# A hand-written issue order for the layer part of a fused decoder kernel

## The chip, the core and the metric

The kernel runs on one core of one Trainium2 chip. The metric is device time in microseconds (us) of one execution; lower is better. A core has five instruction streams that matter here: TensorE (PE in the profile, with its weight loads as PEld), VectorE (DVE), ScalarE (ACT), GpSimd (POOL) and SyncE (SP), which issues most of the transfers. Each stream is worked off in the order in which its instructions stand, and semaphores make one stream wait for another.

## The reference

The input is `x` of shape 8 x 512 x 512 (batch, sequence, width) in 32-bit floats. Three sublayers follow each other, each inside a residual sum and a layernorm:

```python
x = _layernorm(x + mamba(x))                    # _L0_attn_ref
x = _layernorm(x + cross_attention(x, ctx))     # _L0_xattn_ref, 16 heads of 32
x = _layernorm(x + mixture_of_experts(x))       # _L0_ffn_ref, 32 experts, 4 for each token
```

The first is a state-space layer: layernorm, projection to two halves of 1024 channels, a causal convolution of four taps with silu on one half, a projection to `dt`, `B` and `C`, `dt = softplus(...)`, and then for every one of 1024 channels and 16 states the recurrence along the sequence

```python
h = dA_t * h + dBx_t                      # dA = exp(A * dt),  dBx = dt * B * x
y_t = einsum('bdn,bn->bd', h, C_t)
```

followed by a gate with silu of the other half and a projection back to 512. The second is cross attention with softmax over 512 keys. The third routes each token to 4 of 32 experts (each with room for 640 tokens), adds a shared expert, and sums.

## The kernel before

`program` calls three functions, one after the other. `layers` (lines 83 to 1121) does the first two sublayers, the routing and the shared expert; `experts` does the 32 experts; `finish` does the last layernorm. Only `layers` is touched by the change.

**Chunks and steps.** `layers` walks over 16 chunks: 8 batches, 2 chunks of 256 positions each. A chunk has 32 steps, `steps = [(q, g, i) ...]`: channel pair `q`, state group `g`, and one of two channel blocks. I number the steps of a batch 0 to 63. One step holds one piece of the recurrence: `carry` copies the four starting states into `h` (ScalarE, L443); `decays` computes the four exponentials for the next step into one of two buffers `das` (ScalarE, L437); `scan` multiplies (VectorE, L449), runs the scan (VectorE, L453) and saves the end state (L455); `collect` multiplies the states by C (VectorE, L470) and sums over them on TensorE (L474).

**Other work in the same step.** Before `collect`, a step also emits part of the work that prepares the next chunk or finishes the last one: projections with the streamed weights `wm` (L302), the output projection `back` (L503) with its layernorm, the convolution taps (L336), softplus for the next channel pair (`prepare`, L389 to L412), and two runs of silu, each with two loads of ScalarE's function table (L353, L354). It further emits items of a list `side`: the cross attention, the routing and the shared expert of the batch before, and the keys and values of the batch after. An item has a weight, and the list is spread evenly over a batch's steps by these weights. In attention, `maximum` computes scores (L766) and VectorE reduces them (L768); `weigh` computes them again, transposed (L792), and ScalarE exponentiates (L796); `gather` multiplies with the values (L808). The scores of L766 and L792 share two PSUM buffers (pool `l_pss`).

**Work and clearing away.** An item emits its matmuls at once and returns what empties its PSUM result; that is emitted one item later:

```python
    def do(fn, *args, first=False):
        if first:
            dry()
        rest = fn(*args)
        settle()
        if rest:
            left.append(rest)
```

The body of a step, shortened:

```python
            h = carry(t, 2 * q + ci, g)
            ...
                decays(2 * nq + ni, ng, (f if k + 1 < len(steps) else nf)["ready", nq][0], das[(n + 1) % 2])
            scan(t, 2 * q + ci, g, f["ready", q][1], bc, das[n % 2], h)
            ...
            settle()
            collect(2 * q + ci, g, h, bc, py, f)
```

What stands at the `...` between `scan` and `settle()` are the `do` calls of that step. The `settle()` ahead of `collect` empties everything that is still pending, so that in the source all clearing away of a step stands ahead of its L470.

**What sets the order.** The kernel is written against a recording layer that has a scheduler: the source order is a priority, and the scheduler places each instruction of each engine by its own estimate of when inputs and buffers are ready. A few instructions are tied to the source order by hand (`tc.keep_in_program_order` on the silus of L353 and L354). Transfers on SP (weights, the broadcasts `bc` of L378, the rearranged `both` of L418, the attention's small copies) are placed by the scheduler too.

**Buffers named below.** `h` has 4 buffers, `das` 2, `wm` 3 and `wa` (the attention and shared-expert weights, L525) 2; `both` has 2 for each of its two tiles, `bc` 6; `cT`, the context of the next batch (L661), shares one buffer with the attention's output. `xr` (L725), rows of the first sublayer's result, has 2.

Of the kernel before, what the change touches and what calls it, by code (L numbers as in the profile page):

```python
# [1422 lines left out]
def program(tc, a, out):  # L1423
    nc = tc.nc
    with tc.tile_pool(name="dram", bufs=1, space=DRAM) as dram:
        x1d = dram.tile([N, D], F32, name="x1d")
        filld = dram.tile([B, S], F32, name="filld")

        based = dram.tile([N + P, D], F32, name="based")
        xbuf = dram.tile([SLOTS, ROW], F32, name="xbuf")  # L1430
        nc.scalar.preload_act_table_set(LN_EXP)

        with ExitStack() as ctx:
            layers(ctx, tc, a, x1d, filld, based, xbuf)
        with ExitStack() as ctx:
            experts(ctx, tc, a, xbuf, based)
        with ExitStack() as ctx:
            finish(ctx, tc, based, out)
# [31 lines left out]
```

## Time and profile before

| | |
|---|---|
| median of 3 runs | 5567.89 us (5564.01 to 5571.6) |
| the profiled execution: its own time, its span | 5569.36 us, 5567.7 us |
| TensorE busy | 4880.6 us (88%) |
| VectorE busy | 4349.5 us (78%) |
| ScalarE busy | 2592.1 us (47%) |
| GpSimd busy | 569.2 us (10%) |
| first and last start of the scan L453 | 72.2 and 3688.8 us |
| first expert matmul (L1220) | 3963.3 us |

Busy shares are means over the whole span. The kernel has three stretches with different loads: the steps, from 72 to 3692 us; the attention and shared expert of the last batch alone, to 3963 us; experts and last layernorm, to the end. A matmul's duration in the profile overlaps that of its neighbours, so where I need the cost of an operation I use the distance between starts in the timeline.

### The profile page before, as it was taken

The page shows a single profiled execution, that of the slowest core. Times are in us where ns is not written, and L with a number is a line of the kernel's source. Part 1 is how long each engine was busy: PE and PEld are TensorE (multiplying, and loading weights), DVE is VectorE, ACT ScalarE, POOL GpSimd, SP SyncE. Part 2 cuts the span into 40 slices and gives each one's busy share as a digit, 9 for nine tenths or more (in the row PEclk, how much of TensorE's full clock was granted, in tenths as well). Part 3 has the DMA queues.
Part 4 walks back from the last instruction along what each step waited for, and adds up shares of the span by engine and source line. Part 5 has one row for each costly group of instructions (what it writes and reads, how often), then busy time and mean ns, then how long its engine had stood idle before and what let it go on. Part 6 is the DMA issues. An engine that isn't in the chain of part 4 may idle for free. (4 is left out here: it accounts for less than half of the span.)

```text
span 5567.7 us, 60361 instructions
## 1 busy us (share of the span) xinstructions
PE 4880.6 (88%) x19752; PEld 2718.5 (49%) x19752; DVE 4349.5 (78%) x5738; ACT 2592.1 (47%) x5481; POOL 569.2 (10%) x424
## 2 busy tenths in 40 slices
PE   6668889888888988888898898879899999999994
PEld 4334344334434434443443443333577777777773
DVE  6998899989889999898989999864466565555554
ACT  4555555655566455555555656523222222222223
POOL 1000002001100200200020020010111111111111
PEclk8778999999999999999999999989999999999997
DMA  6787355444634634643463454441345454544444
GB/s 187 226 229 211 109 137 176 121 118 143 178 106 112 201 97 129 184 124 108 122 207 98 120 188 113 112 158 45 96 125 126 124 126 119 126 125 120 119 121 145
DMA packets 554282, 769.83 MB, mean 138 GB/s; under 512 B 135754, under 2 KB 268394, under 8 KB 551920
## 3 DMA queue, kind: packets, MB, share of 16 engines
q1 hardware_dynamic: 517952, 677.55, 41.6%
q0 software_dynamic: 33280, 76.90, 7.4%
q10 hardware_dynamic: 2736, 11.54, 0.5%
q8 instruction: 156, 2.56, 0.2%
q14 instruction: 158, 1.29, 0.1%
HBM read 508.68 MB, written 165.05 MB: 121 GB/s over the span
## 5 line engine op out<-in xcount | busy, mean ns | idle before, releaser
L437 ACT ACTIVATE l_da<-both,l_aneg 128x256 f32<-128x256 f32 x2048 | 888.4, 499 | 790.6 <-DVE h L453 745.9
L453 DVE TENSOR_TENSOR_SCAN h<-l_da,h 128x1028 f32<-128x1028 f32 x512 | 1170.0, 2292 | 50.7 <-ACT h L443 27.3
L474 PE MATMUL py<-h,l_twice 128*64 128x256 f32 x4096 | 627.5, 421 | 195.1 <-DVE h L470 194.9
L449 DVE TENSOR_TENSOR h<-both,bc 128x1024 f32<-128x1024 f32 x512 | 617.9, 1214 | 142.5 <-PE py L474 81.6
L470 DVE TENSOR_TENSOR h<-h,bc 128x1024 f32<-128x1024 f32 x512 | 622.6, 1219 | 6.3 <-DMA l_ka<-filld 0.3
L474 PEld LDWEIGHTS py<-h,l_twice 128*64 128x64 f32 x4096 | 292.5, 147 | 568.8 <-issue 237.7
L1220 PE MATMUL ps_h<-xT,w 128*128 128x320 f32 x1536 | 435.6, 433 | 0.0
L766 PE MATMUL ps_s<-l_ka,l_qa 64*128 64x512 f32 x1024 | 314.1, 692 | 137.4 <-DVE mx L768 137.2
L1300 POOL DMA_INDIRECT based<-y,xe x160 | 252.1, 1576 | 1313.5 <-ACT y L1323 571.3
L1241 DVE TENSOR_TENSOR hT<-ps_h,p 128x320 f32<-128x320 f32 x128 | 62.9, 492 | 379.0 <-PE ps_h L1220 379.0
L768 DVE TENSOR_REDUCE mx<-ps_s 128x2 f32<-128x1024 f32 x256 | 310.4, 1216 | 55.4 <-PE ps_s L766 54.7
L1220 PEld LDWEIGHTS ps_h<-xT,w 128*128 128x128 f32 x1536 | 292.2, 190 | 118.2 <-issue 0.4
L792 PE MATMUL ps_t<-l_qa,l_ka 64*128 64x512 f32 x1024 | 299.6, 648 | 20.9 <-ACT eT L796 17.5
L796 ACT ACTIVATE eT<-ps_t 128x1024 f32<-128x1024 f32 x256 | 259.1, 1013 | 110.1 <-PE ps_t L792 109.6
L808 PE MATMUL po<-eT,l_va 128*64 128x512 f32 x1024 | 281.4, 629 | 24.5 <-ACT raw L820 20.8
L641 POOL DMA_INDIRECT xbuf<-x2t,dest x128 | 218.8, 1709 | 814.6 <-DVE dest L635 776.2
L1220 PE MATMUL ps_h<-t,s 128*128 128x320 f32 x1024 | 286.1, 432 | 0.0
L302 PE MATMUL ps_z<-xnT,wm 128*128 128x256 f32 x1024 | 240.9, 389 | 17.4 <-DVE o L512 16.4
L302 PE MATMUL ps_x<-xnT,wm 128*128 128x256 f32 x1024 | 245.6, 394 | 11.1 <-DMA wm<-in_in_proj_w 10.1
L703 PE MATMUL ps_p<-x2T,wa 128*128 128x512 f32 x512 | 243.9, 625 | 11.8 <-DVE hT L883 10.3
L503 PE MATMUL po<-wm,zs 128*128 128x512 f32 x512 | 236.9, 613 | 9.8 <-DVE k L688 5.3
L1220 PEld LDWEIGHTS ps_h<-t,s 128*128 128x128 f32 x1024 | 194.6, 190 | 81.1
(234 smaller groups left out, 7422.5 us busy)
## 6 DMA issues: line engine op xcount, KB each, us to landing
bc<-scr SPq DMA_DIRECT2D x1024, 128.0 KB
w<-in_w SPq DMA_DIRECT2D x93, 1024.0 KB
wm<-in_in_proj_w SPq DMA_DIRECT2D x128, 512.0 KB
xbuf<-zero SPq DMA_DIRECT2D x32, 1362.5 KB
xe<-xbuf SPq DMA_DIRECT2D x32, 1362.5 KB
both<-dt SPq DMA_DIRECT2D x256, 128.0 KB
both<-dtx SPq DMA_DIRECT2D x256, 128.0 KB
wm<-in_out_proj_w SPq DMA_DIRECT2D x64, 512.0 KB
```

Source lines behind the costliest of these rows:

```text
L302: nc.tensor.matmul(ps[:, i, :], w[:, dc, i * P : (i + 1) * P], f["xnT"][:, dc, :], start=(dc == 0), stop=(dc == DC - 1),)
L437: nc.scalar.activation(da[:, n, 1:], dt[:, c % 2, j, :], AF.Exp, scale=aneg[:, c, j, g, m : m + 1])
L449: nc.vector.tensor_tensor(steps, dtx[:, c % 2].unsqueeze(2).to_broadcast([P, 2, NG // 2, T]), bc[0], ALU.mult)
L453: nc.vector.tensor_tensor_scan(flat, da.rearrange("p n t -> p (n t)"), flat, 0.0, ALU.mult, ALU.add)
L470: nc.vector.tensor_tensor(steps, steps, bc[1], ALU.mult)
L474: nc.tensor.matmul(py[j * HP : (j + 1) * HP, c % 2, :], twice, h[:, j * 2 + m, 1:], start=False, stop=(s == (NST // NG - 1, NG // 2 - 1, 1)),)
L766: nc.tensor.matmul(ps[:, j, :], qa[r, lt * P : (lt + 1) * P], ka[r, :], start=True, stop=True)
L768: return lambda: nc.vector.tensor_reduce(mx[:, lt, :].unsqueeze(2), ps, AX.X, ALU.max) and None
L792: nc.tensor.matmul(ps[:, j, :], ka[r, kc * P : (kc + 1) * P], qa[r, :], start=True, stop=True)
L796: nc.scalar.activation(eT, ps, AF.Exp)
L808: nc.tensor.matmul(po[j * 2 * HD : (j + 1) * 2 * HD, :], va[:, kc, i, j * HD : (j + 2) * HD], eT[:, j, :], start=(kc == 0), stop=(kc == SC ...
L1220: nc.tensor.matmul(ps, w[:, n, r * P : (r + 1) * P], x[:, n, :], start=not more and n == 0, stop=n == 1, skip_group_check=more,)
```

## The change

The body of the `layers` call is put under a manual schedule for four of the five streams. Inside it, the instructions of ScalarE, VectorE, TensorE and SP stand in the order in which the source emits them; GpSimd's are still placed by the scheduler. `experts` and `finish` are outside.

```diff
@@ -1431,6 +1431,7 @@
         nc.scalar.preload_act_table_set(LN_EXP)
 
         with ExitStack() as ctx:
+            ctx.enter_context(tc.manual_schedule(engines={mybir.EngineType.Activation, mybir.EngineType.DVE, mybir.EngineType.PE, mybir.EngineType.SP}))
             layers(ctx, tc, a, x1d, filld, based, xbuf)
         with ExitStack() as ctx:
             experts(ctx, tc, a, xbuf, based)
```

No operation is added or removed by the source, and line numbers up to 1433 are the same in both kernels. What moves, as the two built programs show it: TensorE has the same 10518 instructions in nearly the same order; VectorE has the same 5740, but each step becomes L449, L453, L455, then all clearing away of that step, then L470; ScalarE has each step as L443, four L437, then the clearing away, and 83 table loads in place of 136; on SP, transfers that the scheduler had moved ahead stand at their place in the source.

## The prediction

> **What bounds the kernel now.** I read the busy shares first, then the table of windows cut at the scans that begin each batch, then the waits of VectorE, then the timeline of single steps. Columns of the windows: stretch, length, busy us (instructions) of PE, PEld, DVE, ACT, POOL, then granted clock, DMA share, GB/s.
>
> ```profile
> 72.20:433.40 361.20, 235.91 (x964) 120.97 (x964) 341.19 (x339) 192.76 (x457) 22.38 (x12) 0.77 0.77 221
> ...
> 1370.40:1839.40 469.00, 412.92 (x1685) 194.92 (x1684) 425.85 (x499) 268.05 (x564) 43.28 (x29) 0.93 0.48 138
> ...
> 3245.00:3692.00 447.00, 380.92 (x1580) 175.55 (x1578) 403.04 (x433) 241.79 (x515) 34.11 (x21) 0.94 0.46 135
> 3692.00:3963.30 271.30, 229.58 (x736) 93.18 (x737) 106.11 (x205) 65.55 (x86) 31.92 (x35) 0.89 0.33 111
> 3963.30:5567.70 1604.40, 1532.78 (x6258) 1131.10 (x6256) 923.87 (x1721) 453.31 (x978) 252.10 (x160) 0.98 0.48 122
> ```
>
> A middle batch (there are six, 3245.0 - 433.4 = 2811.6 us, 468.6 each) takes 469 us, in which VectorE is busy 426 (91%), TensorE 413, ScalarE 268. VectorE binds, TensorE is close behind, and only some 43 us of a batch are VectorE's idle time: that is all that a better order could win, and TensorE would then bind at nearly the same figure. The experts (1604 us) run on TensorE and are outside the change.
>
> ```profile
> DVE h L449 <- PE py L474: 12.5, 5, 4.9
> DVE h L449 <- DMA both<-dtx: 6.7, 3, 3.3
> DVE xs L336 <- ACT xs L328: 4.7, 3, 2.3
> ...
> DVE mx L768 <- PE ps_s L766: 2.0, 1, 2.0
> ```
>
> These are VectorE's longest waits in the batch 1370 to 1839 (us, times, longest). They are few, because the scheduler fills a wait with something else. Two stretches of its timeline show how:
>
> ```profile
> 2009.43 1.22 DVE L768 TENSOR_REDUCE mx<-ps_s 128x2 f32<-128x1024 f32 x1
> 2010.57 1.66 DVE L336 SCALAR_TENSOR_TENSOR xs<-xp,l_cw,xs 128x256 f32<-128x256 f32 x4
> 2012.15 1.22 DVE L470 TENSOR_TENSOR h<-h,bc 128x1024 f32<-128x1024 f32 x1
> 2013.29 0.48 DVE L336 SCALAR_TENSOR_TENSOR xs<-xp,l_cw,xs 128x256 f32<-128x256 f32 x1
> 2013.68 1.22 DVE L768 TENSOR_REDUCE mx<-ps_s 128x2 f32<-128x1024 f32 x1
> ...
> 2048.17 1.23 DVE L470 TENSOR_TENSOR h<-h,bc 128x1024 f32<-128x1024 f32 x1
> 2049.31 0.69 DVE L409 SCALAR_TENSOR_TENSOR dtx<-dtx,u 128x512 f32<-128x512 f32 x1
> 2050.03 0.69 DVE L410 TENSOR_TENSOR l<-l,dtx 128x512 f32<-128x512 f32 x1
> 2050.64 1.22 DVE L768 TENSOR_REDUCE mx<-ps_s 128x2 f32<-128x1024 f32 x1
> ```
>
> L470 comes out ahead of taps and reductions, and softplus (L409, L410) only once its ScalarE input is there.
>
> **What the skill says.** The Trainium skill, "Perfetto Trace Analysis", section Per-engine timelines, calls ScalarE and VectorE strict FIFO: a waiting instruction holds all behind it. The trace agrees: VectorE's 5738 and ScalarE's 5492 records stand in it in the order in which the program has them. The same page, section Identifying the Most-Contended Engine, takes occupancy as the measure for VectorE; here 91%. "ScalarE: Activation LUTs", section What ACT_TABLE_LOAD costs, gives 1283 ns for a table load, and the trace has that mean; it adds a drain of 1380 ns, which this trace doesn't show (a load at 2000.25 us is followed by L796 at 2001.55).
>
> **The change, step by step.** In the order of issue a step becomes: VectorE L449, L453, L455, clearing away, L470; TensorE the step's matmuls W, then the sum L474. Three ties follow. L474 waits for L470, so TensorE begins the next W only after L470. The clearing away waits for W, or for ScalarE after W, and L470 stands behind it. The next scan waits for L443, which stands on ScalarE behind this step's clearing away. So TensorE and VectorE advance in lockstep, and a step costs its longer engine or a chain through both, where the scheduler could average over several steps.
>
> Costs, by distance between starts (timeline): L449 1.17 us, L453 2.28, L455 0.16, L470 1.14, together 4.75; reduction L768 1.14; a tap 0.40; a 128x512 VectorE operation 0.61; L474 of a step 0.95; L766 or L792 0.955, L808 1.01 an item; a projection or dense item 3.65 (16 matmuls L302 in 3.72); four L437 1.7; L796 0.92; ScalarE's softplus part 3.05.
>
> I summed both engines over each of a middle batch's 64 steps in the new order, and took the larger:
>
> | steps of the batch | VectorE | TensorE | sum of the larger |
> |---|---|---|---|
> | 0-2, 32-34: output projection | 37.7 | 41.4 | 45.9 |
> | 3-7, 35-38: gate projections | 47.2 | 50.8 | 53.8 |
> | 8-18: convolution, keys, queries | 72.7 | 65.2 | 75.9 |
> | 19-31, 39-47: attention | 157.3 | 131.0 | 159.1 |
> | 48-63: output, routing, shared expert | 110.6 | 96.6 | 118.0 |
> | all | 425.5 | 385.0 | 452.7 |
>
> VectorE's sum is the trace's 425.85; TensorE's is at full clock (the batch had 0.93). Chains add to 453:
>
> - Taps in the step of their own convolution (18, 21, 44, 47): sum L474 and projection 4.6, ScalarE's copy and two L328 1.6, six taps 2.4, L470 1.14 make 9.8 against 7.0: 4 x 2.8 = 11.
> - Softplus inside one step (3, 11, 19, 27, 43, 59): its matmul at 2.1, ScalarE to 5.3, where VectorE is free at 3.6: 1.7 five times, and 3.3 in step 3, whose projection comes first: 12.
> - Output projection with layernorm (1-2, 33-34): VectorE reaches L512 when TensorE ends both halves (16.6), then goes on to L470 at 22.2 while TensorE waits: 5 over the table, twice: 10.
> - Two reductions in a step (20, 22, 26, 30, 31): the second L766 needs the PSUM buffer that the first L768 frees at 4.75; then 0.96, 1.14 and 1.14 give 8.2 against 7.0; smaller misfits in others: 9.
> - A dense item that VectorE empties last (10, 49, 57 to 63): L470 waits for item and emptying, 1.3 to 2 each: 12.
> - Table loads: silu steps have 7 to 10 us of ScalarE, and the next L443 stands behind: 6.
> - Layernorm and softmax round trips between the two: 8.
> - Loads that now stand late on SP: `cT` and the first `wa`, 2 MB, behind the store L515 of step 2, need about 9 us at the 221 GB/s of the first row, and step 3 uses them at once: 4; `xr` with 2 buffers for four transposes: 2. SP's in-order issue of the other small copies and `bc` I take at nothing, since they are issued two steps (14 us) ahead; without that cover each late `bc` shows in full at L449.
>
> Sum 74. Against it: where TensorE is late but VectorE isn't tied to it, the next L449 (1.17) is already done, 8 times, 9 us; ScalarE ahead of its step saves some 5. Net 60, so 453 + 60 = 513 us a batch, 44 above 469. Bounds: with every chain hidden 453, 16 below; with no credit and the clock at 0.95 about 535, 66 above. The 53 table loads that disappear (68 us of ScalarE) lie beside a busier VectorE: 0, at most a gain of 1.283 each.
>
> First batch: no attention, VectorE 354 of order-of-issue work, about 370 with ScalarE's silu steps, 16 of chains: 386 against 361, +25 (0 to +50). Last batch: 434 for the larger plus 50: 484 against 447, +37. The attention alone at the end: the same matmul order, bound by TensorE (230 of 271): 0, give or take 20. Experts: 0. Sum: 6 x 44 + 25 + 37 = 326. Against the profiled execution, 5569 + 326 = 5895 us; its time is 1.5 above the median, which changes nothing.
>
> **Rivals.** *The order is better than the scheduler's* (faster). The list is already spread by weight, emptying lags one item, silus no longer interleave with exponentials. For it: 43 us of idle VectorE in a batch, and 453 is below 469. Price: 6 x -16 and about -10 for the ends, 5460 us. It decides if the chains of 74 us overlap down to under 16, that is if VectorE is ahead of TensorE at most reductions. Against it: L470 behind every emptying leaves nothing to do while it waits.
>
> *SP becomes the bound* (slower still). An SP queue in source order stops at each store that waits for a result, with `bc` and `wm` behind it. If one us of each step showed at L449, 512 us more beside part of the chains: about 6250. Against it: most SP waits in the batch shown are short, and the buffers allow issue well ahead.
>
> *It does nothing*: excluded on VectorE and ScalarE, whose order differs throughout; TensorE's hardly does, and if TensorE alone set the pace, the time would stay at 5570.
>
> **How the numbers follow.** Lockstep with chains, 5700 to 6080: 0.80. SP bound, about 6250: 0.07. Better order: 0.10. No difference: 0.03. A measurement of this kernel tells about 0.2% (11 us) from no change. The range from 5640 to 6160 leaves out the faster rival, no change, and the worst of SP. Predicted: 5895.
>
> **What would show it.** In the changed profile a middle batch should last about 513 us with VectorE busy still 426, so near 83%; waits of VectorE for `ps_s` (L768), for `dtx` of ScalarE (L409), for L328 (L336) and for dense results (L897, L883, L688) should grow from a few us to tens in total over the kernel; TensorE should wait more for L470. The experts' stretch stays 1604. ScalarE's busy time falls by some 68. If VectorE's idle time in a batch falls under 43 us, the lockstep argument is wrong; if L449 waits mainly for `bc` or `both`, it is SP.

## The result and the profile after

The changed kernel takes 6776.19 us (median of 4 runs, 6769.52 to 6781.5) against 5565.95 us for the kernel before beside it: a ratio of 1.218, with a 95% interval of 1.217 to 1.220. It is slower by 1210 us. Slower was forecast, but at 5895 us, and the range ended at 6160.

The same cuts as before, at the first scan of each batch (columns: stretch, length, busy us (instructions) of PE, PEld, DVE, ACT, POOL, then granted clock, DMA share, GB/s). First batch, a middle batch, last batch, the last batch's attention alone, experts:

```profile
70.60:518.90 448.30, 266.08 (x1010) 142.08 (x1012) 362.66 (x355) 194.28 (x468) 4.48 (x12) 0.72 0.68 197
...
1772.90:2401.70 628.80, 461.08 (x1684) 211.47 (x1684) 441.54 (x499) 257.67 (x556) 25.11 (x30) 0.85 0.36 103
...
4282.40:4885.20 602.80, 444.14 (x1580) 198.87 (x1581) 422.78 (x457) 235.35 (x511) 21.11 (x18) 0.83 0.35 99
4885.20:5166.40 281.20, 213.53 (x705) 86.63 (x704) 100.38 (x176) 66.83 (x87) 21.14 (x23) 0.86 0.35 110
5166.40:6771.60 1605.20, 1533.72 (x6258) 1131.97 (x6256) 923.81 (x1721) 453.46 (x978) 251.44 (x160) 0.98 0.48 122
```

All of the loss lies in the steps. The six middle batches last from 518.9 to 4282.4 us, 627 each where they lasted 469: 952 us together. The first batch loses 87, the last 156, the attention alone 10, the experts 1. VectorE, busy for 91% of a middle batch before, is busy for 70%, and TensorE, now the busiest engine, for 73%: no engine sets the pace alone any more, and the waits of the engines for each other make up the rest. What VectorE waits for in that batch (us in total, times, longest):

```profile
DVE h L453 <- ACT h L443: 59.3, 20, 9.8
DVE dtx L409 <- ACT dtx L405: 21.5, 7, 7.6
DVE mx L768 <- PE ps_s L766: 20.8, 12, 3.2
DVE o L512 <- PE po L503: 16.3, 4, 8.1
DVE xs L336 <- ACT xs L328: 15.7, 4, 5.5
DVE k L688 <- PE ps_p L703: 8.9, 3, 3.5
DVE hT L883 <- PE ps_p L703: 7.4, 3, 3.8
DVE xr L856 <- PE ps_p L703: 6.4, 3, 2.7
```

And what TensorE's matmuls wait for, in the same batch:

```profile
PE py L474 <- DVE h L470: 120.5, 40, 14.8
```

In the middle batch of the kernel before, VectorE's longest line was 12.5 us, and these two were:

```profile
PE py L474 <- DVE h L470: 11.3, 3, 7.9
```

```profile
DVE h L453 <- ACT h L443: 3.8, 2, 2.0
```

One stretch of the timeline, steps 54 to 56 of that batch, shows how the waits make each other. First TensorE, then ScalarE, then VectorE (start, us, engine, line, operation; in brackets the idle time before it and what ended it):

```profile
2301.62 3.68 PE L703 MATMUL ps_p<-x2T,wa 128*128 128x512 f32 x8
2320.07 1.98 PE L474 MATMUL py<-h,l_twice 128*64 128x256 f32 x8 [14.78 <-DVE h L470]
2321.98 8.41 PE L703 MATMUL ps_p<-x2T,wa 128*128 128x512 f32 x16
2330.33 1.08 PE L474 MATMUL py<-h,l_twice 128*64 128x256 f32 x8
```

```profile
2330.43 0.59 ACT L885 COPY hT<-ps_p 128x512 f32<-128x512 f32 x1 [2.85 <-PE ps_p L703]
2331.04 1.28 ACT L353 ACT_TABLE_LOAD   x1
2332.33 1.91 ACT L353 ACTIVATE hT<-hT 128x2048 f32<-128x2048 f32 x1
2334.25 1.28 ACT L354 ACT_TABLE_LOAD   x1
2335.54 0.20 ACT L443 COPY h<-l_state 128x4 f32<-128x4 f32 x1
```

```profile
2301.23 2.94 DVE L336 SCALAR_TENSOR_TENSOR xs<-xp,l_cw,xs 128x256 f32<-128x256 f32 x6
2304.08 0.28 DVE L546 TENSOR_REDUCE g_m<-ps_l 128x4 f32<-128x128 f32 x1
...
2318.81 1.22 DVE L470 TENSOR_TENSOR h<-h,bc 128x1024 f32<-128x1024 f32 x1
2319.94 1.22 DVE L449 TENSOR_TENSOR h<-both,bc 128x1024 f32<-128x1024 f32 x1
2321.26 2.30 DVE L453 TENSOR_TENSOR_SCAN h<-l_da,h 128x1028 f32<-128x1028 f32 x1
...
2324.74 1.22 DVE L449 TENSOR_TENSOR h<-both,bc 128x1024 f32<-128x1024 f32 x1
2335.77 2.30 DVE L453 TENSOR_TENSOR_SCAN h<-l_da,h 128x1028 f32<-128x1028 f32 x1 [9.82 <-ACT h L443]
```

The routing (L546 to L602) stands whole ahead of one L470, 14.7 us, and TensorE stands still for 14.78. When it may go on, L474 takes 1.98 us instead of 1.08: the clock has halved (in the trace's record of the granted clock it stands at half from 2307.5 to 2324.6 us). The two dense items that follow are late and partly slow, ScalarE's copy of the second is late, two table loads and a silu follow it, and behind them the 0.2 us of L443 without which the next scan can't start: VectorE is idle 9.82 us.

### The profile page after: what moved, and what is told of

Its sections match the earlier page's. It is cut to its first block, busy times and chain, and to the rows that moved or that the text cites. A ratio compares the mean times of both kernels' runs of the same rounds, so it can differ in the third digit from the quotient of the medians.

```text
span 6771.6 us, 60036 instructions
## 1 busy us (share of the span) xinstructions
PE 5260.9 (78%) x19752; PEld 2851.8 (42%) x19752; DVE 4478.3 (66%) x5738; ACT 2519.9 (37%) x5428; POOL 460.9 (7%) x424
## 5 line engine op out<-in xcount | busy, mean ns | idle before, releaser
L453 DVE TENSOR_TENSOR_SCAN h<-l_da,h 128x1028 f32<-128x1028 f32 x512 | 1177.5, 2300 | 507.5 <-ACT h L443 470.6
L474 PE MATMUL py<-h,l_twice 128*64 128x256 f32 x4096 | 711.2, 478 | 981.0 <-DVE h L470 980.2
L437 ACT ACTIVATE l_da<-both,l_aneg 128x256 f32<-128x256 f32 x2048 | 872.1, 498 | 434.2 <-DVE h L453 432.1
L474 PEld LDWEIGHTS py<-h,l_twice 128*64 128x64 f32 x4096 | 299.7, 162 | 1428.5 <-DVE h L470 1247.5
L449 DVE TENSOR_TENSOR h<-both,bc 128x1024 f32<-128x1024 f32 x512 | 623.4, 1218 | 8.4 <-DMA bc<-scr 8.4
L470 DVE TENSOR_TENSOR h<-h,bc 128x1024 f32<-128x1024 f32 x512 | 624.0, 1219 | 5.4
L768 DVE TENSOR_REDUCE mx<-ps_s 128x2 f32<-128x1024 f32 x256 | 309.4, 1219 | 195.1 <-PE ps_s L766 194.8
L792 PE MATMUL ps_t<-l_qa,l_ka 64*128 64x512 f32 x1024 | 319.9, 699 | 46.6 <-DMA l_qa<-nm 21.3
L808 PE MATMUL po<-eT,l_va 128*64 128x512 f32 x1024 | 302.4, 672 | 19.6 <-ACT raw L820 19.4
L302 PE MATMUL ps_z<-xnT,wm 128*128 128x256 f32 x1024 | 283.6, 438 | 30.8 <-DMA wm<-in_in_proj_w 28.8
L703 PE MATMUL ps_p<-x2T,wa 128*128 128x512 f32 x512 | 291.2, 726 | 5.5 <-ACT x2T L870 4.8
L302 PE MATMUL ps_x<-xnT,wm 128*128 128x256 f32 x1024 | 280.3, 435 | 11.7 <-DMA wm<-in_in_proj_w 11.5
L302 PEld LDWEIGHTS ps_z<-xnT,wm 128*128 128x128 f32 x1024 | 222.3, 223 | 101.1 <-issue 53.7
L336 DVE SCALAR_TENSOR_TENSOR xs<-xp,l_cw,xs 128x256 f32<-128x256 f32 x384 | 179.9, 482 | 123.8 <-ACT xs L328 114.7
L302 PEld LDWEIGHTS ps_x<-xnT,wm 128*128 128x128 f32 x1024 | 220.2, 221 | 78.5 <-issue 34.6
```

The source lines that it names most:

```text
L302: nc.tensor.matmul(ps[:, i, :], w[:, dc, i * P : (i + 1) * P], f["xnT"][:, dc, :], start=(dc == 0), stop=(dc == DC - 1),)
L437: nc.scalar.activation(da[:, n, 1:], dt[:, c % 2, j, :], AF.Exp, scale=aneg[:, c, j, g, m : m + 1])
L449: nc.vector.tensor_tensor(steps, dtx[:, c % 2].unsqueeze(2).to_broadcast([P, 2, NG // 2, T]), bc[0], ALU.mult)
L453: nc.vector.tensor_tensor_scan(flat, da.rearrange("p n t -> p (n t)"), flat, 0.0, ALU.mult, ALU.add)
L470: nc.vector.tensor_tensor(steps, steps, bc[1], ALU.mult)
L474: nc.tensor.matmul(py[j * HP : (j + 1) * HP, c % 2, :], twice, h[:, j * 2 + m, 1:], start=False, stop=(s == (NST // NG - 1, NG // 2 - 1, 1)),)
```

## The experiments

Times are medians in us. Losses are against the kernel before run beside them (5560 to 5565). An expectation names readings, that is possible causes with the time and the waits that each would give; the text says which one a run fits.

### Which engine's order costs what

The set of engines in the changed line was the only edit, for example:

```diff
-            ctx.enter_context(tc.manual_schedule(engines={mybir.EngineType.Activation, mybir.EngineType.DVE, mybir.EngineType.PE, mybir.EngineType.SP}))
+            ctx.enter_context(tc.manual_schedule(engines={mybir.EngineType.PE, mybir.EngineType.SP}))
```

TensorE and SP in source order:

> Source order for TensorE and SP only; VectorE and ScalarE are placed by the scheduler again. If the loss of 1210 us comes from the chains between VectorE, ScalarE and TensorE in source order, nearly all of it goes: 5550 to 5700 us, a middle batch 465 to 480. If the late loads on SP make it, most stays: over 6200 us, with VectorE waiting for bc, both or xt.

ScalarE left to the scheduler:

> Source order for VectorE, TensorE and SP; ScalarE is placed by the scheduler. VectorE's wait for L443 (470 us in the changed kernel) should fall under 150 us if the cause is that L443 stands behind the clearing away on ScalarE; the time then falls by 300 to 500 us, to 6300 to 6500. If those 470 us only show that TensorE is late (what is cleared away isn't there sooner), the time stays above 6600 and the wait moves to L768 and L409.

VectorE left to the scheduler:

> Source order for ScalarE, TensorE and SP; VectorE is placed by the scheduler. If L470 behind the clearing away on VectorE is the main tie, TensorE's waits for L470 (980 us) fall to under 400 and the time to 5700 to 6000. If ScalarE's order holds the chain as well, VectorE still waits for L443 and the time stays at 6200 or more.

SP alone, TensorE alone, all but SP, ScalarE alone, VectorE alone:

> Source order for SP alone; the three compute engines are placed by the scheduler. If the 752 us of the run with TensorE and SP come from SP (a queue that stands still at both<-dt, with bc behind it), the time is 6100 to 6350 and VectorE's wait of L449 for bc stays at 300 us or more. If TensorE's order makes them, the time is 5550 to 5700.

> Source order for TensorE alone. TensorE's order differs from the scheduler's mostly in how finely projections are cut into the sums L474. The SP theory: 5560 to 5680 us. The rival, that TensorE in source order makes the 752 us: 6000 or more, with waits of L768 for ps_s over 150 us.

> Source order for ScalarE, VectorE and TensorE; SP is placed by the scheduler. If SP and the lockstep are two limits of which the later counts, taking SP out brings little: 6550 to 6750 us, with TensorE's waits for L470 near 900. If they add up, it brings most of 750: 5950 to 6150.

> Source order for ScalarE alone: 53 fewer table loads, but L443 and the decays behind the clearing away. If ScalarE's order alone holds VectorE back as the tie says, 5650 to 5900 us, with waits of L453 for L443 over 150 us; if it only saves the loads, 5540 to 5570.

> Source order for VectorE alone. If L470 behind the clearing away is enough to tie VectorE and TensorE, 5950 to 6250 us with TensorE's wait for L470 over 500; if it takes TensorE's and ScalarE's source order as well, 5600 to 5850.

| in source order | time | loss |
|---|---|---|
| ScalarE | 5710 | 147 |
| TensorE | 5748 | 188 |
| VectorE | 5802 | 241 |
| SP | 5982 | 421 |
| TensorE, SP | 6317 | 752 |
| ScalarE, TensorE, SP | 6339 | 774 |
| VectorE, TensorE, SP | 6642 | 1077 |
| ScalarE, VectorE, TensorE | 6671 | 1111 |
| all four | 6776 | 1210 |

**SP.** I had priced SP's order at nothing, and it is the dearest single one. In the run with SP alone, SP waits 633 us in all for `dt` (L411; 208 in the kernel before), and VectorE's wait for the broadcasts behind it shows:

```profile
SPq L418 <- DVE dt L411: 632.6, 63, 30.3
```

```profile
DVE h L449 <- DMA bc<-scr: 258.9, 66, 17.0
```

The first line is from SP's waits, the second from VectorE's, of the same run (the kernel before has 14.9 us of the second kind). SP stops at `both<-dt` until softplus is done on VectorE, and the `bc` transfers stand behind it. But this is not the stop behind the longest waits. Eight waits of over 8 us make up 120 of the 259, and seven of these, one to a batch from the second batch on, follow a stop of 14 to 18 us at the store L515, which waits for the end of the output layernorm on ScalarE. The loads `wa` and `cT`, then `both`, then `bc` stand behind it; here SP had stood 17.0 us ahead of L515:

```profile
1534.94 0.37 SPq L515 DMA_DIRECT2D x1d<-o  x1
...
1554.88 2.41 SPq L378 DMA_DIRECT2D bc<-scr  x4
```

```profile
1558.52 2.36 DVE L449 TENSOR_TENSOR h<-both,bc 128x1024 f32<-128x1024 f32 x2 [17.02 <-DMA bc<-scr]
```

How the other waits divide between the stops of SP was not settled. With TensorE in source order as well, VectorE waits 407.6 us for `bc`, and the time fits that run's second reading. Yet leaving SP out of the four saves only 105 us: in the changed kernel L449 waits 8.4 us for `bc`. Where VectorE is late anyway, a late broadcast isn't seen. Of the expectations, the reading "two limits of which the later counts" held for the run without SP; "6100 to 6350" for SP alone was too high, and neither reading of the run with TensorE alone fitted: its loss of 188 us lies between them (VectorE waits 218 us at L449 for L474 there, 82 before).

**ScalarE and VectorE.** VectorE's order alone costs 241 us, on top of TensorE and SP 325, and leaving it out of the four saves 437. In that run, 6339 us, TensorE waits 372 us for L470 and VectorE still 438 for L443: the second reading. VectorE alone fits its second reading too (TensorE waits 246 us for L470, not over 500): L470 behind the clearing away doesn't tie the two engines by itself. ScalarE's order alone costs 147, with 233 us of waits for L443, as the first reading has it, but adds only 22 to TensorE and SP; leaving it out of the four saves 134, though the line with 470 us of waits for L443 is gone. Those waits moved: L768 for `ps_s` from 195 to 267, L409 from 168 to 236, L336 from 115 to 180. That is the second reading.

One part of VectorE's loss is no wait for another engine. In a middle batch VectorE is busy for 440 us where its order alone is that of the source and for 442 in the changed kernel, but for 426 in the kernel before and in the run with TensorE and SP. In the timeline above, L449 starts 1.13 us after a L470 whose result it doesn't read, and L453 starts 1.32 us after the L449 whose result it does read, though both first instructions last 1.22. In source order L453 follows L449 directly in all 512 steps; the scheduler puts another instruction between them in 324, which starts a median 1.135 us after L449. The taps mostly start 0.40 us apart in the kernel before. In source order a tap mostly follows the one whose result it reads, 0.52 us after it, and six of them take 2.85 us up to the start of the next instruction. An estimate from these figures and the prediction's costs (1.17 and 6 x 0.40), for 64 steps and 8 such rows of taps in a batch: 64 x 0.15 + 8 x 0.45 = 13 us, part of it busy time and part short gaps.

### Taking the two ties out of the source

The first edit emits L470 right behind the scan, and leaves L474 where it is; the second emits L443 for the next step together with the decays:

```diff
             scan(t, 2 * q + ci, g, f["ready", q][1], bc, das[n % 2], h)
+            product_c(h, bc)
```

```diff
-            h = carry(t, 2 * q + ci, g)
+            h = hn
...
                 nq, ng, ni = steps[(k + 1) % len(steps)]
+                hn = carry(t if k + 1 < len(steps) else after[1], 2 * nq + ni, ng)
```

> All four engines in source order, but the source emits L470 right after the scan, ahead of what clears away; the matmuls L474 stay where they are. The lockstep theory: L474 no longer waits for the clearing away, TensorE works through, its clock rises from 0.84 to over 0.9, VectorE waits less; a middle batch falls from 628 to 480 to 540 us, the whole to 5750 to 6150. The rival, that the tie through ScalarE (L443 behind its clearing away) is the main one: 6400 or more, with VectorE's wait for L443 as large as before.

> All four engines in source order, L443 of the next step emitted with the decays, L470 left where it was. VectorE's wait for L443 is 59 us a middle batch in the changed kernel. If that wait is a cost of its own, the whole falls by 350 to 470 us (6300 to 6430). If it mostly shows that TensorE is late, because L470 held it, the wait moves to L768, L409 and L336 and the whole falls by 50 to 200 (6580 to 6730).

> All four engines in source order; the source emits L470 right after the scan, and L443 of the next step together with the decays, ahead of what ScalarE clears away. It takes both ties away. If the two ties hold what the run with the early L470 still loses (VectorE's wait for L443 478 us), the time falls from 6324 to 5750 to 5950. If SP's order is a limit of its own near 6300, as the run with TensorE and SP suggests, it stays at 6150 to 6350, and the wait moves to bc at L449.

The same source with SP left to the scheduler:

> Early L470 and early L443 in the source, source order for ScalarE, VectorE and TensorE, SP placed by the scheduler. If SP's order is what is left of the loss (6194 with it), the time falls to 5600 to 5850. If the compute engines' order still makes most of it, 6000 or more.

| source, engines in its order | time | against 6776 |
|---|---|---|
| early L470, four | 6324 | -452 |
| early L443, four | 6594 | -182 |
| both, four | 6194 | -582 |
| both, all but SP | 5998 | -778 |

L470 is the stronger tie. With it early, TensorE's waits for it over the whole kernel fall from 980 to 310 us (lines have shifted: L476 is L474, L459 is L470), and the waits that had held L470 in a middle batch nearly vanish on VectorE (L409 from 21.5 to 3.0, L336 from 15.7 to 1.9):

```profile
PE py L476 <- DVE h L459: 310.2, 133, 12.2
```

```profile
DVE h L453 <- ACT h L443: 66.2, 24, 8.7
...
DVE dtx L409 <- ACT dtx L405: 3.0, 3, 1.5
...
DVE xs L336 <- ACT xs L328: 1.9, 2, 1.3
```

But the wait for L443 stays, and 6324 lies between the two readings: a middle batch takes 565 us at a clock of 0.87, where the lockstep theory had 480 to 540 and over 0.9. Moving L443 alone removes its line wholly and saves 182 us of 470, since other waits take over (L768 195 to 260, L409 168 to 201, L453 for the decays 131): again the second reading. Both together don't bring the kernel back: 6194 lies in the second reading's range, but the sign of that reading is missing, since L449 waits only 13.5 us for `bc`. With SP free too, 435 us of loss are left. In a middle batch of that run (523 us where it was 469) VectorE is busy for 445 us, so 20 of the 54 us are its own longer work; of its waits no line adds up to more than 17.2 us, and which of them would have to go first was not tried. So two readings failed: that the two ties are nearly all of it, and that SP is what is left.

### The clock

The edit adds matmuls with a zero matrix to the open sum, ahead of L474, so that TensorE works while it waits. First in every step, four or two of them:

```diff
+        for _ in range(4):
+            nc.tensor.matmul(
+                py[:, c % 2, :], blank, w_x[:, 0:4, :], start=False, stop=False, skip_group_check=True
+            )
         steps = h.rearrange("p (j m) t -> p j m t", j=2)[:, :, :, 1:]
         nc.vector.tensor_tensor(steps, steps, bc[1], ALU.mult)
```

> The changed kernel with four more 128x256 matmuls of a zero matrix in each step, added to the sum of L474 just ahead of it, so that TensorE works while it waits for L470. They add 1.85 us of work a step at full clock, 947 us in all. The clock theory: half-clock time (195 us in a middle batch) falls under 80, the matmuls of W get shorter by what their halved clock cost them (up to 67 us a batch), and the total rises by far less than 947: it stays within 150 us of 6776 or falls. The rival, that the clock is low without costing anything because TensorE isn't on the chain: the total rises by 300 us or more.

> The same with two of the zero matmuls, 0.93 us a step, 474 us in all. The clock theory: 6550 to 6750 us, half-clock time about 110 us a batch. The rival: 6900 or more.

The half-clock time is read from the trace's record of the granted clock, which has only two values, full and half. A middle batch of the changed kernel has 197 us of it on average; four fillers a step leave 105, two leave 134.

Four a step: 6808 us, 32 more than without. Two: 6755, 21 fewer. The whole-kernel mean of the clock rises from 0.865 to 0.928 and 0.906. So the time with four fits the clock theory, but the half-clock time didn't fall under 80; with two, the time is 5 us above that theory's range. A middle batch takes 637 us with four and 627 with two, as long as without. The time hardly moves, but that can't tell a gain that is spent again on longer work from no gain at all. So I put the fillers only into measured waits: 29 steps whose L474 had waited, from 1.6 to 14.8 us, and in such number that they fit (20 in step 51, 17 in step 54, none in 35 of the 64 steps), in the six middle batches.

> The changed kernel with zero matmuls only in those steps and in such number that they fit into TensorE's measured wait for L470 (114 in a middle batch, six batches; the first and the last have none). Unlike the runs with two or four in every step, they take next to nothing from work on the chain, so what changes is the clock. If the halved clock after a wait is a main part of what the prediction missed (some 114 us a batch), a middle batch falls from 627 by 25 to 50 us, the whole by 150 to 300. If the clock is only a sign of the waits, the batch stays within 8 us and the whole within 50.

6651 us, 126 fewer, a middle batch 608.6 instead of 627.2. The window of the same batch, filled:

```profile
1732.40:2340.00 607.60, 489.58 (x1912) 243.57 (x1912) 441.80 (x498) 258.21 (x556) 25.54 (x30) 0.91 0.37 107
```

There are 228 more records of matmuls and of weight loads, two for each filler, VectorE's work is the same, and the clock is 0.91 instead of 0.85 (half-clock time 109 us instead of 195). Only work was added, and the clock rose; nothing else in that window explains a shorter batch. So the halved clock is a cost of its own, at least 18.6 us a batch. It lies between my two bounds (8 and 25): real, and not the main part. The fillers raise the clock only part of the way to the 0.93 that this batch had before, so the clock's full share is somewhat more; that part is not measured.

### The better source order without a manual schedule

> No manual schedule; the scheduler of the kernel before gets the source with early L470 and L443. If source order as a priority already held L470 back in the kernel before, up to 1% faster (5510 to 5560). If the scheduler finds the same places anyway, 5555 to 5575. If the earlier priority puts L470 ahead of reductions that TensorE waits for, slower, to 5650.

5569 us, a ratio of 1.001 (interval 1.0005 to 1.002). That is the second reading: the scheduler finds nearly the same places whether L470 and L443 stand early or late (L470 starts on average 3.4 us after the start of its scan, against 3.6 in the kernel before and 6.1 in the changed one). No version tried beats the kernel before.

## Why the prediction was wrong

The direction and the mechanism, engines that hold each other up step by step, held; the size was off by a factor of 3.7. A middle batch was forecast at 513 us and took 628.8. Of the 116 us between, 16 are VectorE's busy time (441.5 us, not 425.5) and 100 its waits (187 us, where 513 - 425.5 = 87.5 follow from the forecast). By the prediction's own steps:

**The sum of the larger, 453 us.** VectorE's half came out 16 us longer. Its costs were distances between starts in the scheduler's order, L449 at 1.17 us and a tap at 0.40, and in source order both stand directly ahead of what reads their result: 1.32, and 2.85 for six taps instead of 2.4. TensorE's half was taken at full clock, and the bound at 0.95. The batch ran at 0.85, and the matmuls of L302 had a mean of 438 ns where they had 382 and 386. The Trainium skill, "TensorE: Matmul & The Clock Gate", section What's actually happening, says that throttled is the default and that activity releases it, with a window of about 3.4 us. The changed kernel's trace agrees: but for the last stretch of its record, the granted clock holds a value for whole multiples of 3.41 us, and in the middle batch the eight matmuls of L474 take 1.97 or 1.98 us after each of the 13 waits of over 3 us, but 1.08 or 1.09 after 13 of the 19 waits between 1 and 3 us. The prediction quoted other pages and missed this one: a change that adds idle time on TensorE also slows the matmuls after it, and in lockstep these are on the chain. By the filler run that is at least 18.6 us a batch.

**The chains, 74 us.** Here is the step that failed most: this term was too small, above all in the third tie, the scan behind L443, priced at 6 us and measured at 59. What the terms measured in a middle batch, as VectorE's waits:

| term | predicted | measured |
|---|---|---|
| next scan behind L443 (table loads) | 6 | 59 |
| softplus in one step (L409) | 12 | 21.5 |
| two reductions (L768) | 9 | 20.8 |
| output projection (L512) | 10 | 16.3 |
| taps (L336) | 11 | 15.7 |
| dense items (L688, L883, L856, L897) | 12 | 28 |
| layernorm, softmax (L839, L60) | 8 | 13 |

Each was there, in its place. The two columns don't hold quite the same: the table of the larger already had 452.7 - 425.5 = 27 us in which VectorE waits for longer TensorE work, 8 of them in the output projection, and the measured waits contain these. With these 8 the output projection came nearly as forecast; the other terms were too small by factors of up to 2.3, and the first by ten. The late loads, priced at 6, show at TensorE: 4.2 us for `cT` and 4.0 for `xr`. Of the 13 us in the last row, 5.7 are one wait at L839 with a transfer on SP ahead of it (ScalarE's L837 stood 4.10 us for `total<-raw`).

The third tie, the scan behind L443, was named and then priced only for the table loads. But every step whose TensorE work is late makes ScalarE's emptying late, and that makes the next L443 late: the chain goes from one step into the next, while each of my prices ended at the step's own L470. The waits for L443 can't be added to the others as a cost of their own either, as the early L443 showed (182 us saved of 470). How the 100 us of waits divide stays open. Each alone, and not to be added, the early L470 made a middle batch 63 us shorter, the early L443 19 and the fillers 19.

**The credits, 14 us.** They were taken for VectorE's L449 and for a ScalarE ahead of its step. What came of them was not measured. L449 is indeed done before VectorE stands at the scan, 20 times in the batch for L443, so the measured waits are what was left after it.

**SP at nothing.** Wrong as a price, since SP in source order costs 421 us alone and 105 among the four. The reason given for nothing was that `bc` is issued two steps (14 us) ahead; with SP alone the stop at L515 is itself 14 to 18 us, and the loads behind it come on top. The rival had the right mechanism, a queue that stands at a wait with `bc` behind it, and was wrong that it would set the time: L449's wait for `bc` is 8.4 us.

**First and last batch.** +87 and +156 where +25 and +37 were forecast, with the same wait in front: VectorE waits 44.6 us for L443 in the first and 57.9 in the last. The first batch's clock fell from 0.77 to 0.72, the last one's from 0.94 to 0.83.

**What held.** The attention alone (+10, within the 20 allowed), the experts (1605 for 1604), ScalarE's busy time (72 us less, 68 forecast), TensorE's waits for L470 (195 to 980 us), and the waits named as signs. The faster rival needed the chains to overlap down to under 16 us a batch; VectorE's waits came out at 187.

## What to carry to other kernels

When an order is fixed that puts one engine's emptying ahead of work that another engine waits for, price the loop over two steps, not one: whatever is late leaves its step through the first instruction behind it on each in-order queue, here a 0.2 us copy. Moving that one copy out of the way isn't enough, though: it gave back 182 of 1210 us, because the lateness left through other instructions. Take the cost of an operation in the order that it will have: a distance between the starts of two independent instructions is too short for a pair in which the second reads the result of the first (here 1.17 against 1.32 us). Idle time that was added to TensorE was charged twice here, once as a wait and once as slower matmuls behind it. And effects of queues that wait for each other don't add: an order that costs 421 us alone can give back only 105 when it is taken out of the whole, so single-engine runs and leave-one-out runs are both needed.

## What the runs showed of the hardware

I had not expected that matmuls of zeros, which change no result, would pay for themselves: 114 of them a batch in measured waits made the kernel 126 us faster, at a mean clock of 0.903 instead of 0.865.
